# Loads ahead of the end go on in the last six slots of attention

## The chip, the cores and the metric

The kernel runs on one NeuronCore of a Trainium2 chip. The metric is the device time of that core in microseconds (us): the median of three runs is 3412.16 us (3411.79 to 3413.78). The engines are named as in the profile: PE (TensorE matmul), PEld (its weight load), DVE (VectorE), ACT (ScalarE), POOL (GpSimd) and SP (SyncE, which here only issues DMAs). A "q" behind a name (SPq, POOLq) is the engine's sequencer.

## The reference

Two images of 512 channels and 64 x 64 pixels, in float32. Two layers, each with a residual:

```
x = x + L0(groupnorm(x))     # deformable convolution (DCNv3)
x = x + L1(groupnorm(x))     # attention, batch norm, relu
```

Only the end of layer 1 matters here. With `px` the normalized pixels (4096 per image):

```
q, k    = tanh(px @ Wq.T), tanh(px @ Wk.T)
attn    = softmax(einsum(q, k, align_w))
content = (px + attn @ (px @ Wv.T)) @ Wfc.T + bfc
mean, var over both images and all pixels, for each channel
out     = x + relu(gamma * (content - mean) / sqrt(var + eps) + beta)
```

The batch norm takes its mean and variance over the whole result. So nothing of the output of a channel can be written before the attention of the last pixel for that channel is done.

## The kernel before

Layer 0 comes first and is not touched. In layer 1 each image is cut into eight chunks of 512 pixels (`NCH = 8`, `CH = 512`), taken as four pairs. The attention of a pair runs in 63 slots (`SLOTS`): seven products of nine slots each. A slot multiplies one tile of attention weights with one tile of values, 14 matmuls on PE, and loads the value tile for three slots later on SP's queue (`load_values`, 448 KB, line L1521). Each product ends with `collect`, in which DVE adds the product to the partial results. The order of all instructions is written out by hand (`manual_schedule`): every engine and every queue takes its instructions in the order in which the program emits them.

Finished content is kept in DRAM (`c_d`), except for the last pair of the last image, which stays on chip (`kept`); the residual x lies in DRAM too (`x1_d`). The 512 channels are two halves h = 0 and h = 1. The statistics of the lower half (h = 0) are complete shortly before the end of attention, those of the upper half only after it.

What remains then is a list `waiting` of 32 items (image n, chunk qb, half h), all of the lower half first. An item goes through these steps:

- `fetch` (L1298) loads the residual `xr` (L1301) and the content `cr` (L1305) into two buffers, 512 KB each. Four of the 32 items have their content on chip and load `xr` only.
- `put_out` (L1279) takes the oldest fetched item. ACT applies scale, shift and relu in two instructions (L1284), DVE adds the residual (L1287), and POOL issues the DMA to the output, 512 KB (L1288). The buffer of `xr` goes to the list `free` at once, that of the content after three more `put_out`.
- `refill` (L1294) fetches items, on SP's queue, as long as `free` holds two buffers.

The buffers are pieces of a ring of 38 tiles that attention itself uses for its weights, and four pieces (`spare`) lent from keys and queries. The name `taken` counts the ring pieces that items hold.

In the last pair of the last image, l is the slot within the pair, 0 to 62. From slot 22 to slot 56 each slot may fetch one item, on POOL's queue, if `spare` still has two pieces or if `live + len(taken) + 2 <= 36`. There `live` is the count of ring pieces that attention still holds at slot l, plus six. In slot 57 `batch_norm(0)` turns the statistics of the lower half into scale and shift. The slots 58 to 62 emit one `put_out` each, the slots 60 to 62 a `refill` too. After slot 62 a loop on SP's queue fetches while `len(taken) + 2 <= 34`, then three items are put out around the last `collect`, `batch_norm(1)` follows, four items are fetched into new buffers (`fin`, L1858), and a loop of `put_out` and `refill` finishes (L1861).

After that a small check (L553 to L568) decides whether a general path must be run: POOL builds an identity matrix, PE, DVE and all the sequencers follow. POOL takes it behind its last output DMA.

Of the kernel before, what the change touches and what calls it, by code (L numbers as in the profile page):

```python
# [574 lines left out]
def window_path(ctx: ExitStack, tc: tile.TileContext, t_in: dict, out: bass.AP, far: bass.AP, sums: bass.AP):  # L575
# [666 lines left out]
    with ExitStack() as l1, tc.manual_schedule():  # L1242
# [9 lines left out]
        def piece(name, shape=(P, 2, CH)):  # L1252
            return ring.tile(list(shape), F32, tag="r", name=name)
# [11 lines left out]
        def batch_norm(h):  # L1265

            mv = bnp.tile([P, 2, 2], F32, name=f"bmv{h}")
            for r in range(2):
                nc.vector.bn_aggr(mv[:, r, :], bst[:, 2 * h + r, :, :].rearrange("p a b -> p (a b)"))
            sc, sh = bnp.tile([P, 2], F32, name=f"bsc{h}"), bnp.tile([P, 2], F32, name=f"bsh{h}")  # L1270
            nc.scalar.activation(sc, mv[:, :, 1], AF.Sqrt, bias=eps)
            yield
            nc.vector.reciprocal(sc, sc)
            nc.vector.tensor_mul(sc, sc, gamma[:, 2 * h : 2 * h + 2])
            nc.vector.tensor_mul(sh, mv[:, :, 0], sc)
            nc.vector.tensor_sub(sh, beta[:, 2 * h : 2 * h + 2], sh)
            scales[h] = sc, sh

        def put_out():  # L1279
            n, qb, h, ct, xr = ready.popleft()  # L1280
            ct = kept.pop((qb, h)) if ct is None else ct
            sc, sh = scales[h]
            for r in range(2):
                nc.scalar.activation(  # L1284
                    ct[:, r, :], ct[:, r, :], AF.Relu, bias=sh[:, r : r + 1], scale=sc[:, r : r + 1]
                )
            nc.vector.tensor_add(ct, ct, xr)  # L1287
            nc.gpsimd.dma_start(out_v[n, :, 2 * h : 2 * h + 2, qb * CH : (qb + 1) * CH], ct)  # L1288
            free.append(xr)
            stored.append(ct)  # L1290
            if len(stored) > 3:
                free.append(stored.popleft())

        def refill():  # L1294
            while waiting and len(free) > 1:
                fetch(lambda name: free.popleft(), nc.sync)
# [11 lines left out]
        with ExitStack() as inner:  # L1308
# [6 lines left out]
            def pair_bank(name):  # L1315
                return bank(name).rearrange("p (a s) q -> p a (s q)", a=2)
# [22 lines left out]
            def load_pixels(n, i, queue):  # L1339
                return [load_chunk(n, 2 * i + h, queue) for h in range(2)]  # L1340
# [68 lines left out]
            def load_queries(n, k):  # L1409
                q = query_tile()  # L1410
                for h in range(2):
                    nc.gpsimd.dma_start(q[h * DQ : (h + 1) * DQ], q_d[n][k])
                return q
# [340 lines left out]
            for n in range(NB):  # L1754
                at = Attention(n)
                first = at.chunks[0]

                for i in range(NCH // 2):
                    if 0 < i < 3 or n and i == 0:
                        k = i + 1 if i else 1  # L1760
                        pixels[k] = load_pixels(n, k, nc.gpsimd)
                    pk = pair_bank("pk")
                    for h in range(2):
                        for kb in range(KB):
                            nc.tensor.matmul(  # L1765
                                pk[:, h, :], wkq[:, kb, h : h + 2].rearrange("p h d -> p (h d)"),
                                pixels[i][h][kb // 2][:, kb % 2, :], start=(kb == 0), stop=(kb == KB - 1),
                            )
                    qt = piece("qt", (P, CH))
                    for h in range(2):  # L1770
                        rk, rq = slice(h * DQ, (h + 1) * DQ), slice((1 - h) * DQ, (2 - h) * DQ)
                        nc.scalar.activation(qt[rq], pk[rq, h, :], AF.Tanh)
                        nc.scalar.activation(keys[rk, i, :], pk[rk, h, :], AF.Tanh)
                    nc.scalar.activation(qt, qt, AF.Identity, scale=al)
                    for h in range(2):
                        nc.scalar.dma_start(q_d[n][i][:, h, :], qt[(1 - h) * DQ : (2 - h) * DQ, :])
                    if i == 0:
                        first.q = load_queries(n, 0)
                    if i:
                        psums[i] = sum_pixels(nc.vector, pixels[i])  # L1780
                    for t in range(4):
                        if t % 2 == 0:
                            raw = []
                        raw.append(piece("vform", (P, 2, 4, P)))

                        def between(stage):
                            event = EARLY.get((i, t))
                            if event and stage == 2:
                                for done in at.open:
                                    settle(*done)  # L1790
                                produce(first, *event)
                                at.open = [(first, *event)]
                            step(2)

                        values(t, pixels[i], psums[i], wc, wcs, raw[-1], between)
                        if t in (1, 2) and i + 1 < NCH // 2:
                            for h in range(2):
                                normalize(pixels[i + 1][t - 1][h], 2 * h, *norms[n])
                        if t % 2:
                            g = 2 * i + t // 2  # L1800
                            fill.append(filling(*raw, v_d[n][g], piece if g + 1 == NG else None))
                        if i == 3 and t == 2:
                            for s in range(3):
                                at.fetch(s)
                    pixels.pop(i)
                    psums.pop(i)
                for s in range(LEAD):
                    at.sums(s)
                for s in range(NCH // 2 * SLOTS):
                    if s == 0:  # L1810
                        at.at(-7, first, s)
                    if s == 2:
                        at.at(-3, first, s)
                    at.slot(s)
                    if s < 5:
                        step(2)
                    if n == 0 and s in (92, 94, 96, 98, 101, 103):
                        next(later, None)
                    l = s - (NCH // 2 - 1) * SLOTS
                    if n + 1 < NB:  # L1820
                        if l == 47:
                            pixels[0] = load_pixels(n + 1, 0, nc.gpsimd)
                        if l == 49:
                            wc = value_output()
                        if l == 51:
                            wcs = sum_value_output(wc)
                        if l in (52, 53):
                            for h in range(2):
                                normalize(pixels[0][l - 52][h], 2 * h, *norms[n + 1])
                        if l == 55:  # L1830
                            psums[0] = sum_pixels(nc.vector, pixels[0])
                    elif l > 57:
                        put_out()
                        if l > 59:
                            refill()
                    elif l == 57:
                        for _ in batch_norm(0):
                            pass
                    elif l >= 22:
                        if l == 22:  # L1840
                            room = key_tile()
                            spare = deque((room[:, 0:2], room[:, 2:4], query_tile(), early))
                        live = 6 + sum(last + g >= l for last in (18, 41, 45, 54) for g in range(NG + 1))
                        if len(spare) > 1 or live + len(taken) + 2 <= 36:
                            fetch(lambda name: spare.popleft() if spare else ring_piece(name), nc.gpsimd)
                if n + 1 == NB:
                    while len(taken) + 2 <= 34:
                        fetch(ring_piece, nc.sync)
                    for _ in at.ends.pop():
                        put_out()  # L1850
                    refill()
                    norm = batch_norm(1)
                    next(norm)
                    put_out()
                    next(norm, None)
                at.rest()
# [54 lines left out]
```

## Time and profile before

| what | us |
|---|---|
| median of three runs | 3412.16 |
| the profiled execution, its own time | 3411.23 |
| its span, first to last instruction | 3409.4 |
| last matmul of attention ends | 3320.2 into the span |
| last output DMA is issued | 3398.9 into the span |

| engine | busy us | share of the span |
|---|---|---|
| PE | 3147.5 | 92% |
| PEld | 2260.3 | 66% |
| DVE | 2755.4 | 81% |
| ACT | 1350.9 | 40% |
| POOL | 432.7 | 13% |

Times inside the span are microseconds from its start. A "window" is a stretch of the span; for each, the profile gives the busy time of every engine (with the number of instructions), the granted clock of PE, the share of time in which the 16 DMA engines were busy, and what they moved in GB/s. A share of 1.0 means that the DMA engines had no free time. SP's and POOL's DMAs use the same 16 DMA engines.

### The profile page before, as it was taken

What the parts mean: (1) busy time and instruction counts of PE and PEld (TensorE: products, weight loads), DVE (VectorE), ACT (ScalarE), POOL (GpSimd) and SP (SyncE); (2) the same over time, 40 slices, a digit from 0 to 9 for tenths busy, and PEclk for the clock granted to TensorE, in tenths of its full rate; (3) what the DMA queues carried; (4) which work ended last, traced back from release to release, by engine and by line L of the source; (5) the groups of instructions that cost most, each with busy time, mean ns of one, the idle gap of its engine ahead of it and who ended that gap; (6) DMA issues with size and microseconds to landing.
All of it is one profiled execution on the core that took longest, in us unless ns stands there. A gap on an engine that the chain in (4) does not pass through costs nothing.

```text
span 3409.4 us, 38281 instructions
## 1 busy us (share of the span) xinstructions
PE 3147.5 (92%) x14147; PEld 2260.3 (66%) x14147; DVE 2755.4 (81%) x3830; ACT 1350.9 (40%) x1803; POOL 432.7 (13%) x468
## 2 busy tenths in 40 slices
PE   4789999999999999899999999999899999999990
PEld 2355555555555666687787777887587787787880
DVE  8899999998999568786886977868697786886974
ACT  2577777788777533202213112123211202203114
POOL 2112111211221001101001011000101101001112
PEclk9889999999999999999999999999999999999995
DMA  6333443344233268758658677657867758657778
GB/s 227 104 99 123 134 128 102 100 123 136 90 104 118 91 237 273 240 176 243 181 173 220 193 198 205 200 189 243 262 195 200 205 178 245 179 174 220 246 280 356
DMA packets 238388, 629.98 MB, mean 185 GB/s; under 512 B 28112, under 2 KB 45136, under 8 KB 237168
## 3 DMA queue, kind: packets, MB, share of 16 engines
q1 hardware_dynamic: 182320, 434.21, 39.0%
q0 software_dynamic: 43072, 156.26, 17.9%
q10 hardware_dynamic: 12800, 36.97, 3.0%
q8 instruction: 114, 1.87, 0.2%
q14 instruction: 82, 0.67, 0.1%
HBM read 410.15 MB, written 124.91 MB: 157 GB/s over the span
## 4 chain that ended last, share of the span: by engine, by line
PE 69%; DVE 19%; DMA 6%; issue 3%; ACT 2%; POOL 1%; SPq 0%; ACTq 0%; POOLq 0%; DVEq 0%
PE accy L1535 21%; PE accx L1535 17%; DVE conv L820 10%; PE pS L1442 6%; PE py L1004 6%; PE pq L789 5%; PE pa L984 5%; PE pvy L1693 3%; PE pvx L1693 2%; PE pk L1765 1%; DVE e L1464 1%; DMA early<-in_x 1%; DMA tot<-e 1%; DMA wv<-vform 1%; DMA wv<-vsum 1%
## 5 line engine op out<-in xcount | busy, mean ns | idle before, releaser
L1535 PE MATMUL accy<-tt,v 128*128 128x256 f32 x2016 | 600.6, 380 | 0.9 <-DVE ct L1564 0.6
L1447 ACT ACTIVATE e<-pS 128x1024 f32<-128x1024 f32 x256 | 248.4, 1021 | 726.0 <-PE pS L1442 721.8
L1535 PE MATMUL accx<-e,v 128*128 128x256 f32 x1792 | 471.6, 386 | 0.0
L1535 PE MATMUL accy<-e,v 128*128 128x256 f32 x1792 | 459.9, 379 | 0.0
L820 DVE SCALAR_TENSOR_TENSOR conv<-xn,L_conv_dw_w_sb,conv 128x504 f32<-128x504 f32 (+1 forms) x512 | 409.3, 807 | 35.9 <-ACT conv L814 22.0
L1535 PEld LDWEIGHTS accy<-tt,v 128*128 128x128 f32 x2016 | 382.9, 190 | 55.1 <-DVE tt L1515 1.1
L1535 PEld LDWEIGHTS accx<-e,v 128*128 128x128 f32 x1792 | 333.5, 190 | 121.0 <-issue 80.2
L1535 PEld LDWEIGHTS accy<-e,v 128*128 128x128 f32 x1792 | 340.7, 190 | 46.4
L1514 DVE TENSOR_TENSOR tt<-e 128x256 f32<-128x256 f32 x448 | 187.9, 419 | 177.2 <-PE accy L1535 149.0
L1515 DVE TENSOR_TENSOR tt<-tt,e 128x512 f32<-128x512 f32 x448 | 310.0, 692 | 15.3
L1535 PE MATMUL accx<-tt,v 128*128 128x256 f32 x1008 | 301.0, 380 | 6.5 <-DVE tt L1514 6.4
L984 PEld LDWEIGHTS pa<-bt,patch 96*128 96x128 f32 x2048 | 251.2, 197 | 56.6 <-issue 34.9
L1442 PE MATMUL pS<-q,keys 64*128 64x512 f32 x1024 | 257.8, 622 | 14.9 <-ACT e L1447 14.9
L984 PE MATMUL pa<-bt,patch 96*128 96x128 f32 x2048 | 254.7, 281 | 6.5 <-ACT bt L970 5.6
L970 ACT COPY bt<-pb 96x1024 f32<-96x1024 f32 x124 | 234.6, 2007 | 57.7 <-PE pb L965 55.3
L789 PE MATMUL pq<-in_w,xn 128*128 128x512 f32 x512 | 238.6, 609 | 6.0 <-DVE o L882 3.9
L1004 PE MATMUL py<-dT,L_conv_out_w_sb 128*128 128x512 f32 x512 | 234.7, 602 | 4.7 <-ACT dT L995 4.7
L1540 ACT COPY u<-accx 128x256 f32<-128x256 f32 x56 | 20.8, 372 | 509.8 <-PE accx L1535 507.0
L1535 PEld LDWEIGHTS accx<-tt,v 128*128 128x128 f32 x1008 | 191.8, 191 | 34.2 <-DVE tt L1514 8.1
L877 PE MATMUL po<-om_w_pg,feat 128*128 128x432 f32 x512 | 203.5, 542 | 2.6 <-ACT feat L860 2.5
L995 ACT COPY dT<-pa 32x256 f32<-32x256 f32 x496 | 179.9, 363 | 64.2 <-PE pa L984 55.4
L1456 POOL DMA_DIRECT2D tot<-e x144 | 124.0, 887 | 584.3 <-DVE e L1432 272.6
(245 smaller groups left out, 4329.1 us busy)
## 6 DMA issues: line engine op xcount, KB each, us to landing
v<-wv SPq DMA_DIRECT2D x436, 448.0 KB
tot<-e POOLq DMA_DIRECT2D x176, 512.0 KB, 7.0
patch<-xt SPq DMA_DIRECT2D x256, 192.0 KB
v<-ww SPq DMA_DIRECT2D x56, 448.0 KB
wv<-vform SPq DMA_DIRECT2D x48, 512.0 KB
wv<-vsum SPq DMA_DIRECT2D x48, 384.0 KB
xt<-xj SPq DMA_DIRECT2D x128, 128.0 KB
res<-in_x SPq DMA_DIRECT2D x64, 256.0 KB
```

What stands on the lines that cost most here:

```text
L789: nc.tensor.matmul(pq, xn[:, kb, 1 + 2 * t : 3 + 2 * t, :].rearrange("p r c -> p (r c)"), in_w[:, kb, :], start=(kb == 0), stop=(kb == KB ...
L820: nc.vector.scalar_tensor_tensor(dst, src, wt, dst, ALU.mult, ALU.add)
L877: nc.tensor.matmul(po[:, : 3 * GP], f[:, kb, t * P : (t + 1) * P], om_w[:, kb].rearrange("p a k g -> p (a k g)"), start=(kb == 0), stop=(k ...
L970: copy(bt[:SN].rearrange("s g q d -> s d (g q)")[:, d0 : d0 + 4, :], pb[:SN])
L984: nc.tensor.matmul(pa[:, p], xp[:SN, p, cb * P : (cb + 1) * P], bt[:SN, 4 * cb : 4 * cb + 4, PX * s + p, :], start=True, stop=True,)
L995: copy(dst, src)
L1004: nc.tensor.matmul(py, out_w[:, kb, cb * P : (cb + 1) * P], dT[:, kb, :], start=(kb == 0), stop=(kb == KB - 1))
L1442: nc.tensor.matmul(p[:, a, :], keys[r, i, (2 * u + h) * P : (2 * u + h + 1) * P], c.q[r, qh, :], start=True, stop=True,)
L1447: nc.scalar.activation(e.rearrange("p a q -> p (a q)"), p.rearrange("p a q -> p (a q)"), AF.Exp)
L1514: nc.vector.tensor_sub(t[:, 0], x[:, 1], x[:, 3])
L1515: nc.vector.tensor_add(t[:, 1:3], t[:, 0].unsqueeze(1).to_broadcast([P, 2, HQ]), x[:, 0:3:2])
L1535: nc.tensor.matmul(out, v[:, blk, :], op, start=(first and g == 0), stop=(final and g == NG))
```

## The change

The branch for slots 57 and up is joined with the one for slots 22 to 56. What the slots 57 to 62 did before (batch norm, `put_out`, `refill`) stands at the head of the joined branch, and the conditional fetch on POOL's queue follows it in these slots too.

```
-                    elif l > 57:
-                        put_out()
+                    elif l >= 22:
+                        if l == 57:
+                            for _ in batch_norm(0):
+                                pass
+                        if l > 57:
+                            put_out()
                         if l > 59:
                             refill()
-                    elif l == 57:
-                        for _ in batch_norm(0):
-                            pass
-                    elif l >= 22:
                         if l == 22:
                             room = key_tile()
                             spare = deque((room[:, 0:2], room[:, 2:4], query_tile(), early))
```

The lines after these are not changed:

```
                        live = 6 + sum(last + g >= l for last in (18, 41, 45, 54) for g in range(NG + 1))
                        if len(spare) > 1 or live + len(taken) + 2 <= 36:
                            fetch(lambda name: spare.popleft() if spare else ring_piece(name), nc.gpsimd)
```

## The prediction

> **What bounds the kernel now.** PE is busy 92% of the span, but the change acts only after attention's slot 57, so I read the end by windows.
>
> ```profile
> 3286.00:3292.00 6.00, 6.00 (x30) 5.28 (x29) 2.55 (x5) 0.37 (x1) 0.00 (x0) 1.00 1.02 411
> 3292.00:3312.00 20.00, 20.00 (x94) 17.61 (x93) 17.82 (x30) 7.71 (x12) 0.49 (x1) 1.00 0.52 163
> 3312.00:3315.00 3.00, 3.00 (x15) 2.65 (x14) 2.63 (x3) 2.19 (x4) 1.64 (x3) 1.00 0.79 240
> 3315.00:3321.00 6.00, 5.16 (x24) 4.19 (x23) 1.10 (x2) 2.47 (x5) 0.79 (x2) 1.00 1.02 396
> 3321.00:3330.00 9.00, 0.18 (x2) 0.11 (x2) 7.50 (x9) 3.36 (x6) 2.18 (x3) 0.74 1.00 371
> 3330.00:3342.00 12.00, 0.00 (x0) 0.00 (x0) 8.55 (x13) 8.58 (x14) 2.18 (x3) 0.50 1.03 419
> 3342.00:3396.00 54.00, 0.00 (x0) 0.00 (x0) 23.96 (x25) 27.56 (x39) 15.26 (x21) 0.50 1.02 418
> 3396.00:3409.00 13.00, 0.37 (x1) 0.08 (x1) 1.79 (x4) 0.36 (x1) 1.24 (x3) 0.50 0.14 53
> ```
>
> Until 3320 PE has no gap; from 3315 to 3396 the DMA engines are full; and before that stands a hole of 20 us in which they are half idle, under a full PE. Next, which transfer ends last? ACT in time order:
>
> ```profile
> 3379.91 1.52 ACT L1284 ACTIVATE cr<-cr,bsh,bsc 128x512 f32<-128x512 f32 x2 [3.34 <-issue]
> 3384.84 1.52 ACT L1284 ACTIVATE cr<-cr,bsh,bsc 128x512 f32<-128x512 f32 x2 [3.42 <-DMA cr<-wc]
> 3389.86 1.52 ACT L1284 ACTIVATE cr<-cr,bsh,bsc 128x512 f32<-128x512 f32 x2 [3.50 <-DMA cr<-wc]
> 3394.84 1.52 ACT L1284 ACTIVATE cr<-cr,bsh,bsc 128x512 f32<-128x512 f32 x2 [3.46 <-DMA cr<-wc]
> ```
>
> From 3359.9 on, the last eight items start 5.0 us apart, each when its load lands. An item has two loads, so SP lands one every 2.5 us: 0.524 MB / 2.5 = 210 GB/s, half of 418. The other half is POOL's outputs. SP's last loads are issued like this:
>
> ```profile
> 3372.44 0.32 SPq L1301 DMA_DIRECT2D xr<-wx  x1
> 3374.94 0.32 SPq L1305 DMA_DIRECT2D cr<-wc  x1
> ```
>
> The last was issued at 3374.94 and used at 3394.84: 19.9 us, eight transfers of 2.5. SP keeps eight in flight, and from 3342 its waits are almost all on its own earlier loads, not on buffers. Outputs issued around 3365 take 19.4 us to land, so POOL has eight in flight as well. The end follows from POOL, in time order:
>
> ```profile
> 3392.94 0.73 POOL L1288 DMA_DIRECT2D out<-cr  x1 [4.29 <-DVE cr L1287]
> 3398.89 0.73 POOL L1288 DMA_DIRECT2D out<-cr  x1 [5.23 <-issue]
> 3399.62 0.22 POOL masks.py:197 MEMSET ident_f<- 128x128 f32 x1
> ```
>
> The final check starts behind the last output's issue. So the end is: last load used (3394.84), ACT and DVE, issue at 3398.89, check, branch, 3409.4. That is a fixed 14.56 us after the last load is used. Loads set the end, and they go at half speed because outputs share the engines.
>
> **What the Trainium skill says.** "DMA: Bandwidth & Descriptors", section "Queues, rings and completion order": each DMA engine serves the queues that have work in turn, packet by packet. The trace agrees: 2.5 us per 512 KB on SP's queue while outputs queue up, against 0.524 MB / 418 GB/s = 1.25 us alone. Its section "Issuing engines are not separate DMA queues" says that DMAs from SP and POOL run on the same 16 engines; the windows agree, as the sum stays at 418 to 419 GB/s whoever issues. The section "Anatomy of one DMA — SWDGE (gpsimd) path" gives about 2.0 us plus bytes at 436 GB/s for one DMA from POOL, 3.2 us here; the last output, alone, took 3.1 us.
>
> **The change part by part.**
>
> *What is emitted.* I counted by hand through slots 22 to 62. At slot 56 `taken` is 22 and `live` 13 (37 > 36, no fetch). After it: slot 57 12+22+2 = 36, fetch; 58 11+24+2 = 37, no; 59 10+24+2 = 36, fetch; 60 no; 61 8+26+2 = 36, fetch; 62 no. Three items move, six loads of 512 KB, from SP to POOL. Before, SP fetched two of them in the refills of slots 60 and 61 and the third just after slot 62. The refills now take the next items instead. After slot 62 and its loop the lists have the same length in both kernels (33 ring pieces taken, 9 waiting). So SP has 28 loads in the tail instead of 34, and POOL 6 more. No arithmetic is added.
>
> *Issue.* 6 x 0.53 us on POOL (its loads of before) and up to 6 x 0.50 off SP. POOL is busy 1.64 of 3 us at most here; I cost it at nothing. If POOL were behind, each load would delay an output by 0.53 us.
>
> *Slot 57's fetch: where it lands.* POOL runs ahead of its slot, as far as its buffers allow:
>
> ```profile
> 3280.75 0.53 POOL L1301 DMA_DIRECT2D xr<-wx  x1 [2.02 <-PE accy L1535]
> 3283.77 0.53 POOL L1305 DMA_DIRECT2D cr<-wc  x1 [2.49 <-PE accy L1535]
> 3311.51 0.73 POOL L1288 DMA_DIRECT2D out<-keys  x1 [27.21 <-DVE keys L1287]
> ```
>
> The first two are slot 55's fetch, though slot 55 itself is at 3296. Each waited for PE to release one ring piece, 3.02 us apart, one slot. Then POOL waits 27.21 us for slot 58's output. I put slot 57's two loads at about 3286.8 and 3289.8. The engines are full until 3292, so they finish in the hole (1.05 MB at the free 255 GB/s is 4.1 us). They cost SP nothing later: two of the six loads are gone for free. What is queued behind them on POOL is only slot 58's output at 3311.5, far off. Value tiles share the engines with them: at half share one takes 0.459 MB / 210 GB/s = 2.2 us of the 3.02 of a slot, and from 3279 to 3291 PE ran without a gap in just that state. Cost nothing; if that cover failed, each late tile is lost time one for one.
>
> *Slots 59 and 61.* These stand behind the outputs of slots 59 and 61 in POOL's order (3312.93 and 3315.75), so they start near 3313.7 and 3316.5. The pieces that they need were released by PE slots earlier. Behind them wait the outputs of slots 60 to 62, for about 1.1 us each time. The engines are nearly full there (240, then 396 GB/s), so these four loads only compete.
>
> *The sum.* From 3312 to 3342 the engines moved 240 x 3 + 396 x 6 + 371 x 9 + 419 x 12 = 11,460 (GB/s x us), 11.5 MB, 21.9 transfers. Of SP's 34 loads 21 were issued by 3342.5 and eight were in flight, so 13 had landed; 21 x 2.5 = 52.5 gives 3395.0 for the last (the trace: 3394.84). After the change POOL asks in that stretch for 4 loads and the same 11 outputs, 15, more than half of 21.9. Bounds: POOL gets strictly half, then SP has landed 11, 17 remain, 42.5 us, end of loads 3384.5, gain 10. Or the four loads displace four of SP's, 9 landed, 19 remain, 47.5 us, 3389.5, gain 5. The unknown is how far outputs fall behind. I take the middle, SP 10 and 18 left: 45 us, 3387.0, gain 7.8. Outputs then lag more, and drain after the loads: about 6 are left at 3387, 7.5 us at full rate plus some 2 us, 3396.5, before the check is over (3387.0 + 14.56 = 3401.6). The eight-in-flight limit asks the last output only to wait for the one eight earlier. So the new bound is still the last load, 7.8 us sooner.
>
> Span 3409.4 - 7.8 = 3401.6; the profiled execution's 3411.23 becomes 3403.4, and the median lies 0.93 above it: 3404.4.
>
> **The rivals.**
>
> A. *Loads end sooner* (above), gain 5 to 10: 3402 to 3407, likeliest 3404.4. For it: SP's even 2.5 us pace for 52 us. Chance 0.60.
>
> B. *Only bytes count*: what the hole took, 1.05 MB / 418 = 2.5 us, because outputs fall so far behind that the last one, not the last load, sets the end, or SP loses its early share to POOL. 3409.7, or 3408 to 3411. Against it: outputs drain at 1.25 us once loads are through. Chance 0.20.
>
> C. *The change does little*: slot 57's loads come late (their pieces not released, POOL stuck), all six fall into the full stretch, and SP gains nothing. 3412, within 1. Against: POOL's loads of before never waited past their slot. Chance 0.13.
>
> D. *Slower*: value tiles come late in slots 52 to 62, and PE stops. Each us is paid in full, as everything behind waits for attention. It would be slower than before when the stops add to more than A's 7.8, some 0.7 us in each of 11 slots, and by 0.2% at 14.6. For that a tile must be late by more than its 9 us of lead. Against: the full stretch 3279 to 3291 without a gap. I would expect 3420. Chance 0.07.
>
> **How the numbers follow.** A difference of 0.2% (6.8 us, that is below 3405.3 or above 3419.0) is about what a measurement tells from no change. The likeliest is A's 3404.4. Of A's 0.60 some 0.12 end above 3405.3; some of B's could be better than its own sum, 0.08: faster 0.56. Slower is most of D, 0.06. The rest, 0.38, is same. The range takes A's ends and B: 3400.5 to 3411.0, leaving most of C and D above and a twentieth below.
>
> **What would show it.** Right: two POOL loads between 3285 and 3300, the hole's 163 GB/s up to about 215, PE without gaps to 3320; four more POOL loads between outputs at 3313 to 3318; SP's last issue near 3367, ACT's last item near 3387, outputs still landing after it, the last issue near 3391. Wrong: ACT's last item near 3395 (C), the last output issued long after the last DVE add (B), PE gaps above 0.5 us near 3290 (D).

## The result, and the profile after

The changed kernel takes 3406.75 us in the median against 3412.75 us for the kernel before: 6.0 us less, ratio 0.9982, 95% interval 0.9975 to 0.9989. In a second comparison, with the same kernel on the chip with other experiments, it was 3405.59 against 3413.15, ratio 0.9976 (0.9968 to 0.9983). So it is faster by about 0.2%, 6 to 8 us.

Single executions of either kernel differ by more than that (by up to 10 us), and in the profiles that difference arises before the change acts. In the profiled execution attention's last matmul ended 7.65 us later than in the profile of before, though PE's program up to there is the same; 4.3 of the 7.65 us are there already at the first instruction of DVE on L1515, 1364 us into the span. From the fortieth-last instruction of that line, well ahead of slot 57, to the end of attention's last matmul, all twelve profiles of this document take the same 136.3 to 136.4 us. So nothing that was moved here delayed attention.

PE in time order, the last row of attention, the kernel before and then the changed one:

```profile
3319.57 0.59 PE L1535 MATMUL accy<-tt,v 128*128 128x256 f32 x2
```

```profile
3327.22 0.59 PE L1535 MATMUL accy<-tt,v 128*128 128x256 f32 x2
```

Therefore I compare the ends by the **tail**: from the end of attention's last matmul (3320.16 before, 3327.81 after) to the end of the span. It is 89.2 us before and 80.3 after. Further profiles of the same two kernels gave 88.6 and 81.4. So the tail is steady within about 1 us, and the change takes 7 to 9 us from it.

The windows of the changed kernel, moved by the 7.65 us so that each covers the same work as the one shown of before (the last two excepted):

```profile
3293.65:3299.65 6.00, 6.00 (x30) 5.28 (x29) 2.54 (x5) 0.37 (x1) 1.06 (x2) 1.00 1.02 415
3299.65:3319.65 20.00, 20.00 (x94) 17.62 (x93) 17.82 (x30) 7.70 (x12) 0.48 (x1) 1.00 0.61 216
3319.65:3322.65 3.00, 3.00 (x15) 2.64 (x14) 2.63 (x3) 2.20 (x4) 2.31 (x5) 1.00 0.82 229
3322.65:3328.65 6.00, 5.17 (x24) 4.20 (x23) 1.10 (x2) 2.46 (x5) 2.36 (x4) 1.00 0.99 348
3328.65:3337.65 9.00, 0.18 (x2) 0.11 (x2) 7.51 (x9) 3.36 (x6) 2.20 (x3) 0.60 1.02 394
3337.65:3349.65 12.00, 0.00 (x0) 0.00 (x0) 8.54 (x13) 8.58 (x14) 2.91 (x4) 0.50 1.03 419
3349.65:3396.00 46.35, 0.00 (x0) 0.00 (x0) 24.45 (x26) 27.72 (x39) 14.54 (x20) 0.50 1.03 420
3396.00:3403.65 7.65, 0.37 (x1) 0.08 (x1) 1.16 (x4) 0.00 (x0) 1.24 (x3) 0.50 0.90 365
```

The half-idle 20 us now move 216 GB/s instead of 163: 53 x 20 = 1.06 MB, which is exactly two loads. PE is as busy there as before. And the last window is new: before, the DMA engines were nearly idle from 3396 on, soon after the last load was in (a share of 0.14); now they are busy for some 7 us after it. The moved loads on POOL, in time order:

```profile
3294.45 0.53 POOL L1301 DMA_DIRECT2D xr<-wx  x1 [2.49 <-PE accy L1535]
3297.47 0.53 POOL L1305 DMA_DIRECT2D cr<-wc  x1 [2.49 <-PE accy L1535]
3319.17 0.73 POOL L1288 DMA_DIRECT2D out<-keys  x1 [21.16 <-DVE keys L1287]
3320.59 0.74 POOL L1288 DMA_DIRECT2D out<-early  x1 [0.69 <-DVE early L1287]
3321.32 0.57 POOL L1301 DMA_DIRECT2D xr<-wx  x1
3321.88 0.55 POOL L1305 DMA_DIRECT2D cr<-wc  x1
...
3324.15 0.57 POOL L1301 DMA_DIRECT2D xr<-wx  x1
3324.71 0.55 POOL L1305 DMA_DIRECT2D cr<-wc  x1
```

Less 7.65 these are 3286.8, 3289.8, 3313.7 and 3316.5, the four times that the prediction named. The end, by ACT and POOL in time order:

```profile
3388.84 1.52 ACT L1284 ACTIVATE cr<-cr,bsh,bsc 128x512 f32<-128x512 f32 x2 [3.48 <-DMA cr<-wc]
3393.82 1.52 ACT L1284 ACTIVATE cr<-cr,bsh,bsc 128x512 f32<-128x512 f32 x2 [3.46 <-DMA cr<-wc]
```

```profile
3393.07 0.73 POOL L1288 DMA_DIRECT2D out<-cr  x1 [1.76 <-DMA out<-ct]
3396.90 0.73 POOL L1288 DMA_DIRECT2D out<-cr  x1 [3.10 <-DVE cr L1287]
```

ACT still starts the last items 5.0 us apart, each when its load lands, so loads at half rate still set the pace. But the last one is used 66.0 us after attention instead of 74.7. The output before the last now waits for an older output, not for DVE: outputs queue up behind the loads.

### The profile page after: what moved, and what is told of

It reads as the page before. It is cut to its first block, busy times and chain, and to the rows that moved or that the text cites. A ratio compares the mean times of both kernels' runs of the same rounds, so it can differ in the third digit from the quotient of the medians.

```text
span 3408.1 us, 38286 instructions
## 1 busy us (share of the span) xinstructions
PE 3153.3 (93%) x14147; PEld 2262.0 (66%) x14147; DVE 2755.2 (81%) x3830; ACT 1350.6 (40%) x1803; POOL 436.1 (13%) x474
## 4 chain that ended last, share of the span: by engine, by line
PE 70%; DVE 19%; DMA 6%; ACT 2%; issue 2%; POOL 1%; SPq 0%; ACTq 0%; POOLq 0%; DVEq 0%
PE accy L1535 22%; PE accx L1535 17%; DVE conv L820 10%; PE pS L1442 6%; PE py L1004 6%; PE pq L789 5%; PE pa L984 5%; PE pvy L1693 3%; PE pvx L1693 2%; DMA wv<-vform 1%; PE pk L1765 1%; DMA early<-in_x 1%; DVE e L1464 1%; DMA tot<-e 1%; PE p_mean L836 1%
## 5 line engine op out<-in xcount | busy, mean ns | idle before, releaser
L1515 DVE TENSOR_TENSOR tt<-tt,e 128x512 f32<-128x512 f32 x448 | 309.9, 692 | 15.3
```

What stands on the lines that cost most here:

```text
L1515: nc.vector.tensor_add(t[:, 1:3], t[:, 0].unsqueeze(1).to_broadcast([P, 2, HQ]), x[:, 0:3:2])
```

## The experiments

All numbers but the last column are from the profiles, in us after the end of attention's last matmul. "Last item" is the start of ACT on it, which is when its load has landed. "Landed" is the issue of the last output plus its time to landing. "Branch" is the duration of PE's branch in the final check (L570). The ratio is that of the medians of the execution times, with its 95% interval.

| run | loads in the half-idle stretch | last item | last output issued | landed | branch | tail | ratio |
|---|---|---|---|---|---|---|---|
| before | 0 | 74.7 | 78.7 | 81.8 | 3.56 | 89.2 | |
| e10_before_again | 0 | 73.8 | 77.9 | 81.0 | 3.82 | 88.6 | |
| after | 2, and 4 on POOL later | 66.0 | 69.1 | 76.9 | 4.20 | 80.3 | 0.9982 (0.9975 to 0.9989) |
| e8_after_again | the same | 65.5 | 68.6 | 76.5 | 4.68 | 81.4 | 0.9976 (0.9968 to 0.9983) |
| e1_only57 | 2 | 68.5 | 71.6 | 75.6 | 3.96 | 82.5 | 0.9978 (0.9968 to 0.9988) |
| e2_only59_61 | 0, 4 on POOL later | 71.0 | 74.1 | 79.2 | 3.62 | 84.7 | 0.9991 (0.9985 to 0.9998) |
| e3_sp | 4, on SP | 64.9 | 68.9 | 74.4 | 3.93 | 79.3 | 0.9976 (0.9966 to 0.9987) |
| e7_two57 | 4 | 62.4 | 65.5 | 73.8 | 5.10 | 78.8 | 0.9967 (0.9955 to 0.9979) |
| e5_hole | 8 | 56.7 | 60.1 | 71.1 | 6.13 | 74.4 | 0.9958 (0.9944 to 0.9971) |
| e6_fin_pool | 0, 8 on POOL later | - | 69.6 | 81.2 | 6.36 | 85.0 | 0.9996 (0.9987 to 1.0004) |
| e4_fin_act | 0, 8 on ACT later | - | 78.4 | 81.8 | 3.46 | 88.8 | 1.0000 (0.9994 to 1.0007) |

In the last two, loads do not set ACT's last start, so none is given. Each line rests on one profile, and a tail came again within about 1 us, so differences of 1 us between tails say nothing.

### The fetch of slot 57 alone

Against the changed kernel:

```
-                        if len(spare) > 1 or live + len(taken) + 2 <= 36:
+                        if l <= 57 and (len(spare) > 1 or live + len(taken) + 2 <= 36):
```

> The fetch in slot 57 alone is kept, so two loads move into the stretch in which the DMA engines are half idle, and no load joins POOL's queue between the outputs. Measure beside the time: the tail, from the end of attention's last matmul to the end of the span, 89.2 us in the kernel before and 80.3 in the changed one. Theory (loads set the end, and while outputs share the engines each load costs 2.5 us): SP has 32 loads instead of 34, gain 2 x 2.5 = 5.0 us, tail about 84.2. Rival (only bytes count): 1.05 MB at 418 GB/s, gain 2.5 us, tail about 86.7. Rival (the slot-57 fetch does nothing): tail 89.

Measured: tail 82.5, 6.7 us less than before (6.1 less than the second profile of before); by the medians 4.1 to 10.9 us. Two loads are worth more than their bytes, which would be 2.5. The last item came 6.2 us earlier (5.3 against the second profile), 2.7 to 3.1 us for each load. About half a us of the 6.7 is not theirs: the last output was issued 3.1 us after the last item's start instead of 4.1, for a reason that no view names ("issue"), and the branch took 0.4 us longer. So most of the gain of the whole change is this one fetch.

### The fetches of slots 59 and 61 alone

```
-                        if len(spare) > 1 or live + len(taken) + 2 <= 36:
+                        if (l < 57 or l in (59, 61)) and (len(spare) > 1 or live + len(taken) + 2 <= 36):
```

> The fetches of slots 59 and 61 alone are kept: four loads move from SP's queue to POOL's, all in or next to the stretch in which the DMA engines are full, and none into the half-idle stretch. Theory (loads set the end; loads in POOL's queue push outputs back, not SP's loads): gain between 0 (each displaces one load of SP) and 10, by the changed kernel's 8.9 less 5.0 for slot 57 about 3.9, tail about 85.3. Rival (only bytes count): no byte leaves the full stretch, gain 0, tail about 89.2.

Measured: tail 84.7, gain 4.5; by the medians 0.7 to 5.1 us. No byte left the full stretch (the half-idle 20 us carry 164 GB/s here, 163 before), and still there is a gain, so "only bytes count" is wrong here too. Four loads that change from SP's queue to POOL's bring SP's last load forward by 3.7 us (2.8 against the second profile of before), 0.7 to 0.9 for each. In its place outputs land later relative to the loads: the last one took 5.1 us from issue to landing instead of 3.1, in time that used to be idle.

### The same fetches on SP's queue

```
-                            fetch(lambda name: spare.popleft() if spare else ring_piece(name), nc.gpsimd)
+                            fetch(lambda name: spare.popleft() if spare else ring_piece(name), nc.gpsimd if l < 57 else nc.sync)
```

> All three fetches as in the changed kernel, but issued on SP's queue instead of POOL's. The fetch of slot 57 then stands behind the value tile issued at about 3302 (times as in the profile of before), that of slot 59 behind the last value tile at about 3308, so four loads instead of two run in the half-idle stretch; that of slot 61 runs at about 3316 in the full one, on SP. Theory (loads set the end at 2.5 us each): four loads leave the full stretch, 17 left at 3342 instead of 21, gain 10 us, tail about 79. Rival (the gain of the changed kernel comes from the queue on which the loads stand, not from the time): 4 x 1.25 = 5 us at most, tail about 84. Rival (value tiles behind the loads in SP's queue come late): gaps of PE near slots 61 and 62, longer attention.

Measured: tail 79.3, as the theory had it, and not 84; by the medians 4.4 to 11.6 us less than before. The profile shows no gap of PE up to the end of attention. The gain of slot 57's fetch comes from the time at which the loads run, not from POOL's queue. On SP the loads do not stand behind outputs, so the fetch of slot 59 reaches the half-idle stretch as well: in windows moved like those above, the 20 us carry 243 GB/s, three loads more than before (1.6 MB), and the 3 us after them 281 instead of 240, a part of the fourth.

### The last four fetches on ACT's queue

Against the kernel before:

```
-            fetch(lambda name: fin.tile([P, 2, CH], F32, tag="f", name=name), nc.sync)
+            fetch(lambda name: fin.tile([P, 2, CH], F32, tag="f", name=name), nc.scalar)
```

> The kernel before with one edit: the four fetches into the last buffers, eight loads of 512 KB that are issued after attention, go on ACT's DMA queue instead of SP's. No load starts earlier than 3338, so no byte leaves the full stretch. Theory (queues with work share the DMA engines in equal parts, and loads set the end): with two load queues beside the outputs, loads get two thirds for about 30 us: 8 on ACT and 8 on SP at 3.75 us each, then some 5 more on SP at 2.5, last load at about 3384.5, gain 8 to 10 us, with outputs landing after the last load; tail about 80. Rival (only bytes count): gain 0, tail about 89.

Measured: no difference. But the edit did something else than it was meant to. ACT in time order:

```profile
3335.79 1.50 ACT L1284 ACTIVATE cr<-cr,bsh,bsc 128x512 f32<-128x512 f32 x2
3348.91 0.33 ACTq L1301 DMA_DIRECT2D xr<-wx  x1
...
3363.76 0.33 ACTq L1305 DMA_DIRECT2D cr<-wc  x1
3364.14 7.16 ACT L1284 ACTIVATE cr<-cr,bsh,bsc 128x512 f32<-128x512 f32 x10 [26.85 <-DMA cr<-wc]
```

ACT takes its DMAs in the order of its program, and each waited for an earlier load to land: in the trace the loads of SP and of ACT take the same eight semaphores in turn (107, 109, 111 to 116), each one free again when the load eight before it has landed. So ACT stood still for 26.85 us, and no item was put out meanwhile; nor did a second queue bring more loads into flight, eight in all as before. This does not test the shares of the queues. It shows one thing: with all loads pulled ahead of the outputs, the last output landed at 81.8, where it landed before.

### The last four fetches on POOL's queue

The same edit with `nc.gpsimd` in place of `nc.scalar`.

> The kernel before with one edit: the four fetches into the last buffers, eight loads, go on POOL's queue instead of SP's, ahead of the tenth output. No load starts earlier than in the kernel before and ACT issues nothing, so ACT can't be held up by it. Theory (SP's loads at half rate set the end, so loads taken off SP's queue bring it forward, until outputs are the bound): SP has 26 loads, its last lands some 20 us sooner, outputs lag by eight transfers, are the last to land at about 3396, and the branch follows: gain 6 to 9, tail 80 to 83. Rival (only bytes that leave the full stretch count): gain 0, tail about 89.

Measured: tail 85.0, gain 4.2 instead of 6 to 9; by the medians nothing that can be told from zero (4.4 us faster to 1.4 slower). The last output was issued 9.1 us sooner, as expected, but landed at 81.2, only 0.6 sooner. All of the gain is that the final check now runs beside the landing outputs: 3.8 us remain after the last landing, where it was 7.4 before. The edit also held POOL's outputs up for 10 us in the middle (none was issued between 3340.0 and 3350.2 of its span): POOL's DMAs take eight semaphores of their own in turn (99 to 106), and loads and outputs now shared them. So outputs are a second bound, close behind the loads: what leaves SP's queue without leaving the full stretch only trades one for the other.

### Two items, and four, into the half-idle stretch

Against the changed kernel, two items in slot 57 and none later:

```
-                        if len(spare) > 1 or live + len(taken) + 2 <= 36:
+                        if l == 57:
+                            for _ in range(2):
+                                fetch(ring_piece, nc.gpsimd)
+                        elif l < 57 and (len(spare) > 1 or live + len(taken) + 2 <= 36):
```

> Slot 57 fetches two items on POOL's queue, and slots 58 to 62 none: four loads in the half-idle stretch instead of the two of the run with slot 57 alone (which gave a tail of 82.5), and none between the outputs. Theory: 2.5 us for each of four loads, gain 10, tail about 79. Rival (only bytes count): 1.25 us each, gain 5, tail about 84.

Three items in slot 57 on POOL's queue, and one in slot 59 on SP's:

```
+                        if l == 57:
+                            for _ in range(3):
+                                fetch(ring_piece, nc.gpsimd)
+                        elif l == 59:
+                            fetch(ring_piece, nc.sync)
+                        elif l < 57 and (len(spare) > 1 or live + len(taken) + 2 <= 36):
```

> Slot 57 fetches three items at once on POOL's queue, slot 59 one more on SP's queue; nothing else is fetched in slots 57 to 62 but by the refills. Eight loads instead of two run in the half-idle stretch ahead of the outputs. Theory (each load that leaves the full stretch is worth 2.5 us while loads set the end): up to 20 us, tail 69; but what is left by then, 29.7 MB at 420 GB/s, ends at about 3386, and some 4 us of branch follow, so outputs become the bound at a tail of about 70 to 72. Rival (only bytes count): 8 x 1.25 = 10 us, tail about 79. Rival (value tiles are starved by six loads in a row): gaps of PE between 3287 and 3310.

Measured: tails 78.8 and 74.4. The ring has room for this, since `live` holds a reserve of six. The windows and the last issues of the run with four items:

```profile
3292.00:3312.00 20.00, 20.00 (x94) 17.61 (x93) 17.16 (x30) 5.28 (x9) 2.64 (x5) 1.00 0.93 356
...
3384.00:3390.00 6.00, 0.37 (x1) 0.08 (x1) 0.56 (x3) 0.00 (x0) 0.29 (x1) 0.50 1.02 419
```

```profile
3381.80 0.72 POOL L1288 DMA_DIRECT2D out<-cr  x1 [0.57 <-DMA out<-ct]
3383.03 0.72 POOL L1288 DMA_DIRECT2D out<-cr  x1 [0.51 <-DMA out<-ct]
```

The stretch is now nearly full, PE has no gap in it, and the engines stay full past the last issue. This window stands 2.8 us earlier in the work than those above; moved like them it shows a share of 0.92 and 337 GB/s, and the 3 us after it 337 instead of 240. Together that is some 7 loads more than before (3.8 MB), not quite the eight. The tail of 74.4 is above the 70 to 72 that were expected: the branch took 6.1 us, where some 4 had been put. That run is faster than both kernels: 3398.61 us in the median of five executions, 0.9958 of before.

The three doses give the shape of the effect. For 2, 4 and 8 loads the last item comes 6.2, 12.3 and 18.0 us earlier, 3.1, 3.1 and 2.3 each. But the tail shrinks by 6.7, 10.4 and 14.8: 3.4 for each of the first two loads, 1.9 for each of the next two, 1.1 for each of the last four (by the medians 3.5, 2.1 and 0.8). With tails good to about 1 us, the first two figures are uncertain by half a us or more. The last figure is close to what the bytes alone are worth, 1.25 us.

### Traffic beside PE's branch

Against the kernel before, at its very end:

```
         while ready:
             put_out()
             refill()
+        for t in list(free)[-2:-14:-2]:
+            nc.sync.dma_start(t, x1_d[0][0][:, 0:2, :])
```

> The kernel before with six more loads of 512 KB on SP's queue that nothing uses, issued when DVE is through with the last item: they keep the DMA engines busy for about 7.5 us from some 77.5 us after attention's end, over PE's branch of the final check (L570), which begins 82 us after it. In the kernel before that branch takes 3.56 us with nothing else on the DMA engines, and it took 4.2 to 6.4 us in the runs in which outputs were still landing. Theory (the branch is lengthened by DMA traffic beside it): 5 us or more here. Rival (it depends on the outputs, or on the place in time): 3.5 to 3.7. The whole time is longer by the loads and says nothing.

PE's branch in the kernel before, then with the extra traffic, then in the run with the last four fetches on POOL (duration in ns, min/median/max, then its start):

```profile
L570 PEldq COMPARE_BRANCH  x1: 3558/3558/3558, 3401.9 to 3401.9; - x1
```

```profile
L570 PEldq COMPARE_BRANCH  x1: 6415/6415/6415, 3402.6 to 3402.6; - x1
```

```profile
L570 PEldq COMPARE_BRANCH  x1: 6355/6355/6355, 3395.3 to 3395.3; - x1
```

The branch takes 6.4 us instead of 3.6 with loads beside it that nothing waits for. So it is DMA traffic that lengthens it, not the place in time. The outputs as such do not either: the last output of this run, slowed by the loads, landed 1.4 us after the branch had ended, so the branch did not wait for it.

The traces also show what it most likely does wait for. Among the DMA queues the profile lists q8, of the kind "instruction". In each of the twelve profiles a packet of 16 KB begins on it soon after the branch does: 1.05 us after it in the kernel before, 4.07 us with the extra traffic. And in all twelve the branch ends 1.3 to 1.4 us after that packet has landed, whether it takes 3.5 us or 6.4. So the branch follows a fetch of instructions by DMA, and what the traffic delays is this fetch. That is read from the traces; no run removed the fetch.

### Both kernels once more

> The kernel before once more, for a second profile of its end. If the tail is steady whatever the time of the part before it, it is 89.2 us within 1 us, the last output lands 81.8 us after attention's end, and PE's branch takes 3.5 to 3.6 us.

> The changed kernel once more, beside the others on one chip. If the tail of its first profile, 80.3 us, is its own, it comes again within 1 us, whatever the time of the part before it; if that tail was chance, it lies between 80 and 86, the value that the medians of the first comparison (6.0 us apart) would give being 83.

Measured: 88.6 and 81.4. The tail of before came again within 1 us, with a branch of 3.8 us where 3.5 to 3.6 were expected; that of the changed kernel just missed it (80.3, then 81.4), with the branch 0.5 us longer the second time. Between these four profiles the gain is 7.2 to 8.9 us.

## Why the prediction was right

**The place.** The steps before the sum held: which slots fetch (57, 59, 61), POOL's times, the 1.06 MB in the half-idle stretch (216 GB/s; "about 215" was predicted), value tiles without delay, no cost of issue that shows.

**Loads set the end.** "18 left to land at 2.5 us" was right: 22.3 us after attention's end, 18 of SP's 28 loads were issued and eight in flight, so 10 had landed, as assumed. The last item was used at 3393.82 - 7.65 = 3386.2, against 3387.0 predicted. But the 10 was the middle between two bounds, taken without a reason of its own, and that it came out so exactly was luck. The DMA packets show what lay behind it: in the 30 us that the working adds up SP moved 10.9 transfers of 512 KB and POOL 10.6, against 13.7 and 8.0 before. So POOL took its full half, which is the first bound ("strictly half"); that bound put SP's landed loads at 11 because it did not allow for a load that is under way. The working also starts the 18 loads at 3342.0, where it had started the 21 of the kernel before at 3342.5; this adds half a us to the gain.

**The sum.** 7.8 us was predicted, from a tail of 89.2 to 81.4; the two profiles have 80.3 and 81.4, the medians 6.0 and 7.6. The line of 0.2% (6.8 us), beyond which the prediction gave 0.56 to "faster", lies between these two medians: the direction is clear, the side of that line is not. The two halves of the sum were not so well sized, and their errors cancelled. For the two loads of slot 57 the working implies 2 x 2.5 = 5.0; alone they gave 6.7. For the four loads on POOL's queue the rest, 2.8; beside slot 57's they gave 1.1 to 2.2, though 4.5 alone. They compete for the same idle time at the end.

**"A fixed 14.56 us after the last load is used".** This step fails. It was 14.3 and 15.9 us in the changed kernel, 16.4 with four loads and 17.7 with eight in the half-idle stretch. The steps behind the last item are no longer alone on the DMA engines: PE's branch took 4.2 and 4.7 us instead of 3.6. In the changed kernel that costs 0.6 to 1.1 us, and about 1 us came back because the last output was issued 3.1 us after the last item's start instead of 4.1; so the forecast hardly moved. Further on it costs more: 3.1 us of what eight loads gain.

**The rivals.** "Only bytes count" (B) is refuted as a whole by the runs with slot 57 alone and with slots 59 and 61 alone, and its reason, that outputs set the end, becomes true where more is moved: from four to eight loads each is worth its bytes. "The change does little" (C) is refuted by the two loads in the half-idle stretch. "Slower" (D) is refuted by PE without a gap even at 337 GB/s, and by the 136.3 us that attention's last part takes in every profile.

Why two loads brought the last item forward by 2.7 to 3.1 us each and not by 2.5 can be counted in the packets. From 8 us ahead of attention's end to the last item, the kernel before moved 34 loads on SP's queue and 30.0 transfers on POOL's. With slot 57's fetch alone it was 32 and 27.2: 4.85 transfers fewer, times 1.25 is 6.1 us, and 6.2 was measured. With two items in slot 57 it was 30 and 24.3, 12.2 us, measured 12.3. So for each load that was taken away, about 1.4 outputs fell behind the last load, where the prediction's half speed implies one. Why it is 1.4 stays open.

## What to carry to other kernels

Where a phase that keeps PE full is followed by one that keeps the DMA engines full, look for idle DMA time under the first, and move loads there; what it is worth is read from what paces the second phase. A load that shares the engines with a second queue costs two transfers' time, so while loads set the end, taking one away is worth twice its bytes (here a little more); once the other queue drains last, it was worth about its bytes here. And moving a transfer to another queue shifts that balance even if it moves in time by nothing, but it can also stop the engine that issues it.

## What the runs showed of the hardware

- PE's branch at the end takes 3.5 to 3.8 us with idle DMA engines and up to 6.4 us beside full ones, and in all twelve profiles it ends 1.3 to 1.4 us after a 16 KB packet of the queue for instructions has landed. A chain of small steps after the last transfer is not of fixed length.
- With two queues full, 512 KB take 2.5 us on each, over 50 us at a stretch in the kernel before, and at the same pace in every run in which loads set the end. This is the taking of turns that the Trainium skill describes ("DMA: Bandwidth & Descriptors", section "Queues, rings and completion order").
- Eight loads on ACT's queue stopped ACT's arithmetic for 26.85 us.
- The limit of eight DMAs in flight, which the prediction read off for SP and for POOL, is the program's: each has eight semaphores that its DMAs take in turn, and ACT's loads share those of SP.
